# Step sizes with tiles of their own in the second layer of a two-layer kernel

## The chip, the cores and the metric

The kernel runs on one core of a Trainium2 chip. The metric is the device time of one execution in microseconds (us). Five engines work side by side, each through its own list of instructions in order: PE (matmul, with its weight loads shown apart as PEld), DVE (vector work), ACT (activation functions and copies), POOL (a second, slower vector engine) and SP, which here only issues DMAs. An instruction that must wait holds up everything behind it on its engine. SBUF is the on-chip memory of 128 partitions, PSUM the banks that PE writes to.

## What is computed

Two layers run one after the other over x of 16 x 512 x 128. The first holds a state-space mixer and a routed feed-forward part; it is not touched. The second adds to x an attention with hierarchical levels and a recurrent cell over the 16 blocks. What matters here is how the attention forms its step sizes dt and its level weights Lam:

```python
xn = _layernorm(x, axis=-1)
V  = (x @ Wv.T).reshape(Bb, Tt, H, HD)
dl = (x @ Wdl.T).reshape(Bb, Tt, H, LV)
A = -jnp.exp(A_log)
dt = jax.nn.softplus(x @ Wdt.T + dt_bias)
g = A[None, None, :] * dt
Lam = jax.nn.softplus(Lp[None, None] * dl)
cg = jnp.cumsum(g, axis=1)
diff = cg[:, :, None, :] - cg[:, None, :, :]
decay = jnp.exp(jnp.where(tri[None, :, :, None], diff, NEG))
...
Wmat = scores * jnp.transpose(decay, (0, 3, 1, 2)) * jnp.transpose(lam_ts, (0, 2, 1, 3))
Y = jnp.einsum('bhts,bshd->bthd', Wmat, V).reshape(Bb, Tt, H * HD)
```

Here x inside the attention is xn, and lam_ts picks from Lam the level of each pair of positions. There are 16 heads.

## The kernel before

The work is cut into 16 blocks of 512 positions, held as 128 partitions by 4 groups. Blocks of the second layer have tiles named b_..., those of the first layer other names; some first-layer tiles borrow the space of second-layer tiles (lent_...).

The order on each engine is not that of the source. Every operation is recorded by the class Plan, with its dependences, a guessed duration and a base time of its stage. The method flush then walks the list backwards, gives every operation a key (the smaller the more urgent) from its base time and the longest guessed chain behind it, and places operations engine by engine, always the ready one with the smallest key. Two things in the key matter here. First, weights in the tables URGENT and STAGES (in thousands of ns) go by engine and by the name of the tile that is written: "s:b_sp": -3.0 puts off ACT's writes to b_sp, "g:b_sp": 0.5 and "v:b_sp": 1.0 hurry those of POOL and DVE, "v:b_small": -1.0 and, in the stages 16 to 21, "v:b_gr": -8.0 put off DVE's writes to those tiles. Second, each operation gets a random part of up to 50 ns either way from one generator, drawn in that backward walk. All operations are issued from line 479, so the profile shows L479 for all of them, and they are told apart by their tiles.

The second layer's loop (from line 1365 on) runs over the blocks. In one pass block b goes through states, diagonal, products, upper, upper2 and diagonal2, the next block through gates and factors, the one before through finish:

- gates(b), line 978: the projections b_pp (PE) are copied by ACT to vz, whose first 128 columns of each group are V and whose other 176 columns are z. Of these 176, columns 96 to 111 are the step sizes of 16 heads, the other 160 the level weights. V goes out to the DRAM tile dV and comes back in four DMAs as vbd. The softplus of all 176 x 4 = 704 columns is formed in one go: on ACT u = |z|, u = exp(-u), sp = ln(1 + u); on DVE sp = max(z, 0) + sp and z = (u + 1) - 1; on POOL u = u - z and sp = sp + u, a correction for what 1 + u rounds away. For small u the step sizes take a series (ser) in place of the logarithm, put in by a copy_predicated with the mask small. Then gg = dt * A, its three bf16 parts in g3, exp(gg) back into the step columns of sp, and there times a mask tmask.
- factors(b), line 1042: b_pe, 30 small bf16 matmuls per pass that sum g3, then ACT's b_ex = exp(pe); b_la, ten small products of ex and sp on DVE; b_pld, four transposes of sp, from which ACT and DVE make ldr and ld3, and these go through DRAM (dde, dld) to come back as dd and R.
- states(b), line 1125: bv = V * ex, the matmuls b_pG, and a DVE and ACT chain that fills Gs. upper(b, q), line 1166: the matmuls b_pU of four heads with Gs and th_all, copied to b_yq. products(b), line 1233: 16 heads of three matmuls b_pT each, copied by ACT to th_all. diagonal and diagonal2, lines 1207 and 1243: the scans into b_dec, the multiplies by b_pl (from R) and by b_pS, then b_pyd. finish(b), line 1269: the output projection b_po, a layer norm (b_lc_...) and the store.

The tiles of the softplus have one buffer each, vz has two. A new block's tile waits until the block before has read the old one.

Of the kernel before, what the change touches and what calls it, by code (L numbers as in the profile page):

```python
# [12 lines left out]
F32 = mybir.dt.float32  # L13
F32R = mybir.dt.float32r
BF16 = mybir.dt.bfloat16
AF = mybir.ActivationFunctionType
ALU = mybir.AluOpType
# [6 lines left out]
P = 128  # L24
NG = 4
NH = 16
# [56 lines left out]
class Plan:  # L83
# [100 lines left out]
    def act(self, *args, **kw):  # L184
        i = self.record("scalar", "activation", args, kw)
        self.ops[i].deps.add(self.table)
        self.group.append(i)
        return i
# [304 lines left out]
def two_layer_kernel(ctx: ExitStack, tc: tile.TileContext, a: dict, out: bass.AP):  # L493
    nc = Plan(tc.nc, tc)
# [5 lines left out]
    sp = ctx.enter_context(tc.tile_pool(name="s", bufs=1))  # L500
# [7 lines left out]
    def bank(name, tag="tr", shape=(P, 512), dt=F32):  # L508
        return nc.bank(ps, shape, dt, tag, name)

    def bt(shape, dt, tag, name, bufs=None):
        return nc.tile(sp, shape, dt, tag, name, bufs or BUFS.get(tag, 1))

    def wt(shape, dt, name):
        return wp.tile(list(shape), dt, tag=name, name=name)
# [13 lines left out]
    def mm3(o, lh, ll, rh, rl, start=True, stop=True):  # L529
        nc.tensor.matmul(o, lh, rh, start=start, stop=False)  # L530
        nc.tensor.matmul(o, lh, rl, start=False, stop=False)
        nc.tensor.matmul(o, ll, rh, start=False, stop=stop)

    act = nc.act
# [9 lines left out]
    one_c = wt([P, 1], F32, "one_c")  # L544
# [100 lines left out]
    tmask = pk0[:, 134:135]  # L645
# [11 lines left out]
    nA, dtb = rows[:, 0:16], rows[:, 16:32]  # L657
# [35 lines left out]
    for e in range(8):  # L693
# [9 lines left out]
        op=ALU.mult,  # L703
# [264 lines left out]
    def namer1(b):  # L968
        return lambda s: f"b_{s}_{b}"
# [8 lines left out]
    def gates(b):  # L978

        n, d = namer1(b), B[b]  # L980
        xh, xl = d["xh"], d["xl"]
        vz = bt([P, NG, 304], F32, "vz", n("vz"))
        d["V"], z = V, z = vz[:, :, 0:128], vz[:, :, 128:304]
        d["hh"] = hh = bt([P, NG, P], F32, "hh", n("hh"))
        for g in range(NG):
            pp = bank(n(f"pp{g}"), "pj")
            sl = slice(g * P, (g + 1) * P)
            mm3(pp[:, :NP], xh[:, sl], xl[:, sl], wpj_h, wpj_l)
            nc.scalar.copy(vz[:, g, :], pp[:, 0:304])
            if b:  # L990
                nc.vector.tensor_tensor(hh[:, g, :], pp[:, 304:432], cfo[:, g, :], op=ALU.add)
            else:
                nc.vector.tensor_copy(hh[:, g, :], pp[:, 304:432])

        dV = nc.tile(dram, [NG, NG, C, P], F32, "dV", n("dV"), 2)
        nc.sync.dma_start(dV.rearrange("g j s c -> (j s) g c"), V)
        if b < 2:
            vbd.append(bt([P, NG, NG, P], F32, "vbd", n("vbd")))
            nc.vector.memset(vbd[b], 0.0)
        for g in range(NG):  # L1000
            nc.sync.dma_start(vbd[b % 2][g * C : (g + 1) * C, :, g, :], dV[g].rearrange("j s c -> s j c"))

        nc.vector.tensor_tensor(
            z[:, :, 96:112], z[:, :, 96:112], dtb.unsqueeze(1).to_broadcast([P, NG, NH]), op=ALU.add
        )
        u = bt([P, NG, 176], F32, "u", n("u"))
        d["sp"] = sp = bt([P, NG, 176], F32, "sp", n("sp"))
        act(u, z, AF.Abs)
        act(u, u, AF.Exp, scale=-1.0)
        act(sp, u, AF.Ln, bias=one_c)  # L1010
        dtv = sp[:, :, 96:112]

        ud = u[:, :, 96:112]
        ser = bt([P, NG, NH], F32, "ser", n("ser"))
        small = bt([P, NG, NH], mybir.dt.uint8, "small", n("small"))
        nc.vector.tensor_scalar(small, ud, 2.0**-7, None, op0=ALU.is_lt)
        nc.vector.tensor_scalar(ser, ud, 1.0 / 3.0, -0.5, op0=ALU.mult, op1=ALU.add)
        nc.vector.tensor_tensor(ser, ser, ud, op=ALU.mult)
        nc.vector.scalar_tensor_tensor(ser, ser, 1.0, ud, op0=ALU.add, op1=ALU.mult)
        nc.vector.scalar_tensor_tensor(ser, z[:, :, 96:112], 0.0, ser, op0=ALU.max, op1=ALU.add)  # L1020
        nc.vector.scalar_tensor_tensor(sp, z, 0.0, sp, op0=ALU.max, op1=ALU.add)

        nc.vector.tensor_scalar(z, u, 1.0, -1.0, op0=ALU.add, op1=ALU.add)
        nc.gpsimd.tensor_tensor(u, u, z, op=ALU.subtract)
        nc.gpsimd.tensor_tensor(sp, sp, u, op=ALU.add)
        nc.vector.copy_predicated(dtv, small, ser)
        gg = bt([P, NG, NH], F32, "gg", n("gg"))
        nc.vector.tensor_tensor(gg, dtv, nA.unsqueeze(1).to_broadcast([P, NG, NH]), op=ALU.mult)

        g3 = bt([P, 3, NG, NH], BF16, "g3", n("g3"))  # L1030
        gr = bt([P, NG, NH], F32, "gr", n("gr"))
        nc.vector.tensor_copy(g3[:, 0], gg)
        nc.vector.tensor_tensor(gr, gg, g3[:, 0], op=ALU.subtract)
        nc.vector.tensor_copy(g3[:, 1], gr)
        nc.vector.tensor_tensor(g3[:, 2], gr, g3[:, 1], op=ALU.subtract)

        act(dtv, gg, AF.Exp)
        nc.vector.tensor_scalar(dtv, dtv, tmask, None, op0=ALU.mult)

        d["g3"] = g3  # L1040

# [252 lines left out]
    for i in range(-2, NB + 3):  # L1294
# [26 lines left out]
        if i == NB - 1:  # L1321
            gates(0)
            load1(1)
# [39 lines left out]
    for b in range(NB + 1):  # L1363
        nc.base = (NB + 4) * PA + (b + 1) * PB
        nc.start_group(LNEXP)
        if 0 < b < NB:
            states(b)
        if b + 2 < NB:
            load1(b + 2)
        if b + 1 < NB:  # L1370
            gates(b + 1)
        if b:
            finish(b - 1)
        if b < NB:
            if b:
                diagonal(b)
            for q in range(4):
                if b:
                    products(b, heads=range(4 * q, 4 * q + 4))
                if q:  # L1380
                    upper(b, q - 1)
        if b + 1 < NB:
            factors(b + 1)
        if b < NB:
            upper(b, 3)
            upper2(b)
            diagonal2(b)
        if b + 1 < NB:
            nc.start_group(EXPTANH)
            cell_out(b + 1)  # L1390
# [113 lines left out]
```

## Time and profile before

| | |
|---|---|
| Median of 3 runs | 829.51 us (827.62 to 831.28) |
| Profiled execution | 828.71 us |
| Its span, first to last instruction | 826.5 us |
| Granted PE clock, mean | 0.985 |
| First layer, last cell matmuls | up to 328 us |
| Second layer, first b_pp | 276.3 us |
| Second layer, first softplus | 281.3 us |
| Second layer, last softplus | 760.5 us |

The span is the time from the first to the last instruction; the rest of the 828.71 us lies around it. A busy share says how much of the span an engine worked. The chain that ended last is followed back from the last instruction, at each step to what released it. A line of a tile's view gives engine, operation, written and read tiles, count, and the minimum, median and maximum duration in ns, then the first and last start in us and the shape. A line of a chain or timeline gives start and length in us.

### The profile page before, as it was taken

The numbers are of one execution on the slowest core, as the hardware profiler recorded it, in microseconds if no ns is written. First come the engines' busy times: TensorE is split into PE (matmuls) and PEld (weight loads), VectorE is DVE, ScalarE is ACT, GpSimd is POOL, SyncE is SP. The second block draws the span as 40 slices with busy tenths as digits, with TensorE's granted clock in tenths as the row PEclk, the third lists the DMA queues.
The fourth block names the chain that finished last, engine by engine and source line by source line (L and its number), as shares of the span: only waits on it lengthen the run. The fifth ranks groups of instructions, "written<-read, shape, count | busy, mean of one in ns | idle before, by whom it ended". The sixth has DMA issues, their size and how long they took to land.

```text
span 826.5 us, 27744 instructions
## 1 busy us (share of the span) xinstructions
PE 790.8 (96%) x11432; PEld 605.4 (73%) x11432; DVE 735.5 (89%) x1889; ACT 631.9 (76%) x1322; POOL 206.7 (25%) x236
## 2 busy tenths in 40 slices
PE   7899999999999998999999999999999999999994
PEld 4577878777888776787677778768677778677772
DVE  5799999999998996798989999888999989899885
ACT  6788898989898887876696697587588577587573
POOL 2200000000000110333343343533433523433521
PEclk9799999999999998999999999999999999999998
DMA  9516444334333334254345346435346426536311
GB/s 226 132 52 205 141 154 127 103 113 136 112 109 108 109 115 139 78 135 117 104 128 147 96 130 150 130 94 151 100 123 158 136 79 156 130 87 157 88 52 40
DMA packets 92402, 100.18 MB, mean 121 GB/s; under 512 B 26532, under 2 KB 63788, under 8 KB 90156
## 3 DMA queue, kind: packets, MB, share of 16 engines
q1 hardware_dynamic: 92276, 98.41, 42.5%
q8 instruction: 90, 1.47, 0.7%
q14 instruction: 36, 0.29, 0.1%
HBM read 63.70 MB, written 34.67 MB: 119 GB/s over the span
## 4 chain that ended last, share of the span: by engine, by line
PE 56%; DVE 18%; ACT 15%; DMA 4%; issue 3%; POOL 3%; SPq 0%; ACTq 0%; DVEq 0%; POOLq 0%
PE b_pT L479 11%; PE pg L479 6%; DVE b_dec L479 5%; ACT th_all L479 5%; PE b_pU L479 5%; PE po L479 5%; PE pm L479 4%; PE b_pY L479 3%; PE b_pS L479 2%; DVE b_la L479 2%; PE pC L479 2%; ACT L479 2%; PE pxi L479 2%; PE pz L479 2%; PE b_pp L479 2%
## 5 line engine op out<-in xcount | busy, mean ns | idle before, releaser
L479 ACT COPY th_all<-b_pT 128x512 f32<-128x512 f32 x256 | 145.0, 622 | 25.9 <-PE b_pT L479 20.0
L479 PE MATMUL b_pT<-b_xh,A_h 128*128 128x512 f32 x256 | 108.1, 422 | 1.2 <-DVE b_tiles L479 0.9
L479 POOL TENSOR_TENSOR b_u<-b_u,b_vz 128x704 f32<-128x704 f32 x16 | 27.9, 1743 | 298.7 <-DVE b_vz L479 256.9
L479 PE MATMUL b_pT<-b_xh,A_l 128*128 128x512 f32 x256 | 100.8, 394 | 0.0
L479 PE MATMUL b_pT<-b_xl,A_h 128*128 128x512 f32 x256 | 100.4, 392 | 0.0
L479 ACT ACT_TABLE_LOAD x71 | 91.1, 1283 | 1.9 <-PEq L1494 0.7
L479 DVE TENSOR_TENSOR_SCAN b_dec<-b_dd,upat 128x512 f32<-128x512 f32 x64 | 77.8, 1226 | 4.5 <-PE b_pyd L479 3.0
L479 PEld LDWEIGHTS b_pU<-th_all,Gs 128*32 128x32 f32 x4096 | 61.3, 110 | 19.2 <-issue 9.0
L479 PE MATMUL b_pU<-th_all,Gs 128*32 128x64 f32 x4096 | 70.9, 220 | 2.1 <-ACT th_all L479 0.9
L479 PE MATMUL b_pS<-th_all,b_xf 128*32 128x512 f32 x512 | 60.3, 594 | 0.4 <-ACT th_all L479 0.4
L479 PEld LDWEIGHTS b_pT<-b_xh,A_h 128*128 128x128 f32 x256 | 48.1, 188 | 15.3 <-PE b_pT L479 1.3
L479 PEld LDWEIGHTS b_pT<-b_xh,A_l 128*128 128x128 f32 x256 | 48.1, 188 | 10.9
L479 PEld LDWEIGHTS b_pT<-b_xl,A_h 128*128 128x128 f32 x256 | 48.3, 189 | 6.9
L479 ACT COPY b_yq<-b_pU 128x512 f32<-128x512 f32 x64 | 38.5, 614 | 13.8 <-PE b_pU L479 13.4
L479 DVE TENSOR_TENSOR b_dec<-b_dec,b_pl 128x512 f32<-128x512 f32 x64 | 40.3, 680 | 9.4 <-PE b_pl L479 9.4
L479 DVE TENSOR_TENSOR b_dec<-b_pS,b_dec 128x512 f32<-128x512 f32 x64 | 43.6, 681 | 1.2 <-PE b_pS L479 1.0
L479 DVE TENSOR_TENSOR b_la<-b_ex,b_sp 64x32 f32<-64x32 f32 (+3 forms) x160 | 41.4, 284 | 1.7
L479 ACT ACTIVATE lent_vbd_x<-lent_vbd_x,lb_nb,lb_r 128x128 f32<-128x128 f32 x64 | 29.6, 489 | 11.8 <-DVE lb_nb L479 8.7
L479 DVE TENSOR_TENSOR b_aY<-b_pY,b_la 128x384 f32<-128x384 f32 (+1 forms) x64 | 33.9, 543 | 4.4 <-POOL b_ysum L479 3.0
L479 PE MATMUL pg<-lent_yq_x1h,lent_hh_w 128*128 128x512 f32 x96 | 33.8, 431 | 1.1 <-DVE lent_yq_x1h L479 1.1
L479 PE MATMUL pm<-Gs,ww 128*128 128x512 f32 x64 | 34.5, 621 | 0.0
L479 ACT ACTIVATE b_o<-b_o,b_lc_nb,b_lc_r 128x128 f32<-128x128 f32 x64 | 33.7, 552 | 0.9 <-DVE b_lc_nb L479 0.9
(268 smaller groups left out, 2154.7 us busy)
## 6 DMA issues: line engine op xcount, KB each, us to landing
b_dd<-b_dde SPq DMA_DIRECT2D x64, 256.0 KB, 5.7
b_dld<-b_ld SPq DMA_DIRECT2D x48, 96.0 KB, 2.8
b_R<-b_dld SPq DMA_DIRECT2D x16, 288.0 KB
d_x<-lent_vbd_x SPq DMA_DIRECT2D x16, 256.0 KB, 3.4
d_xt<-lent_vbd_x SPq DMA_DIRECT2D x16, 256.0 KB, 3.7
b_xt<-d_xt SPq DMA_DIRECT2D x16, 256.0 KB, 3.7
d_xf<-th_all SPq DMA_DIRECT2D x16, 256.0 KB, 2.0
d_xh<-lent_yq_x1h SPq DMA_DIRECT2D x16, 256.0 KB, 3.6
```

The source lines that it names most:

```text
L479: o.inst = getattr(getattr(self.nc, o.eng), o.name)(*o.args, **o.kw)
```

## The change

The step sizes get tiles of 64 columns: zd for the biased input, ud for exp(-|zd|), dtv for the softplus. Their three ACT functions, the max-and-add and the correction are recorded before those of the 704 columns, and their correction is on DVE. The softplus of all 704 columns stays as it was, the step columns among them, but z no longer gets the bias, and the step columns of sp are overwritten at the end by exp(gg) times the mask. gg and gr lose their own tiles and use zd and ud. The series, the mask small, g3 and everything outside gates stay as they were.

```diff
-        nc.vector.tensor_tensor(
-            z[:, :, 96:112], z[:, :, 96:112], dtb.unsqueeze(1).to_broadcast([P, NG, NH]), op=ALU.add
-        )
-        u = bt([P, NG, 176], F32, "u", n("u"))
-        d["sp"] = sp = bt([P, NG, 176], F32, "sp", n("sp"))
-        act(u, z, AF.Abs)
-        act(u, u, AF.Exp, scale=-1.0)
-        act(sp, u, AF.Ln, bias=one_c)
-        dtv = sp[:, :, 96:112]
-
-        ud = u[:, :, 96:112]
+
+        zd = bt([P, NG, NH], F32, "zd", n("zd"))
+        nc.vector.tensor_tensor(zd, z[:, :, 96:112], dtb.unsqueeze(1).to_broadcast([P, NG, NH]), op=ALU.add)
+        ud = bt([P, NG, NH], F32, "ud", n("ud"))
+        dtv = bt([P, NG, NH], F32, "dtv", n("dtv"))
+        act(ud, zd, AF.Abs)
+        act(ud, ud, AF.Exp, scale=-1.0)
+        act(dtv, ud, AF.Ln, bias=one_c)
+
...
-        nc.vector.scalar_tensor_tensor(ser, z[:, :, 96:112], 0.0, ser, op0=ALU.max, op1=ALU.add)
-        nc.vector.scalar_tensor_tensor(sp, z, 0.0, sp, op0=ALU.max, op1=ALU.add)
-
-        nc.vector.tensor_scalar(z, u, 1.0, -1.0, op0=ALU.add, op1=ALU.add)
-        nc.gpsimd.tensor_tensor(u, u, z, op=ALU.subtract)
-        nc.gpsimd.tensor_tensor(sp, sp, u, op=ALU.add)
+        nc.vector.scalar_tensor_tensor(ser, zd, 0.0, ser, op0=ALU.max, op1=ALU.add)
+        nc.vector.scalar_tensor_tensor(dtv, zd, 0.0, dtv, op0=ALU.max, op1=ALU.add)
+
+        nc.vector.tensor_scalar(zd, ud, 1.0, -1.0, op0=ALU.add, op1=ALU.add)
+        nc.vector.tensor_tensor(ud, ud, zd, op=ALU.subtract)
+        nc.vector.tensor_tensor(dtv, dtv, ud, op=ALU.add)
         nc.vector.copy_predicated(dtv, small, ser)
-        gg = bt([P, NG, NH], F32, "gg", n("gg"))
+        gg, gr = zd, ud
         nc.vector.tensor_tensor(gg, dtv, nA.unsqueeze(1).to_broadcast([P, NG, NH]), op=ALU.mult)
...
-        gr = bt([P, NG, NH], F32, "gr", n("gr"))
...
         act(dtv, gg, AF.Exp)
-        nc.vector.tensor_scalar(dtv, dtv, tmask, None, op0=ALU.mult)
+
+        u = bt([P, NG, 176], F32, "u", n("u"))
+        d["sp"] = sp = bt([P, NG, 176], F32, "sp", n("sp"))
+        act(u, z, AF.Abs)
+        act(u, u, AF.Exp, scale=-1.0)
+        act(sp, u, AF.Ln, bias=one_c)
+        nc.vector.scalar_tensor_tensor(sp, z, 0.0, sp, op0=ALU.max, op1=ALU.add)
+        nc.vector.tensor_scalar(z, u, 1.0, -1.0, op0=ALU.add, op1=ALU.add)
+        nc.gpsimd.tensor_tensor(u, u, z, op=ALU.subtract)
+        nc.gpsimd.tensor_tensor(sp, sp, u, op=ALU.add)
+        nc.vector.tensor_scalar(sp[:, :, 96:112], dtv, tmask, None, op0=ALU.mult)
```

## The prediction

> **What bounds the kernel now.** I read first the busy shares and the chain that ended last, both over the whole span of 826.5 us.
>
> ```profile
> PE 790.8 (96%) x11432; PEld 605.4 (73%) x11432; DVE 735.5 (89%) x1889; ACT 631.9 (76%) x1322; POOL 206.7 (25%) x236
> ...
> PE 56%; DVE 18%; ACT 15%; DMA 4%; issue 3%; POOL 3%; SPq 0%; ACTq 0%; DVEq 0%; POOLq 0%
> ```
>
> The reader is to see that PE carries most of the chain, DVE is nearly as full, and POOL, which the change relieves of a place in a chain and not of work, holds 3%. The changed code runs from about 281 us on, so the second view is the steady part of the second layer, twelve blocks of 31 us.
>
> ```profile
> 382.00:754.00 372.00, 364.14 (x7275) 279.69 (x7275) 338.20 (x831) 273.08 (x546) 150.44 (x174) 1.00 0.48 127
> ```
>
> The columns are length, then busy PE, weight loads, DVE, ACT and POOL. PE is idle for 372 - 364.1 = 7.9 us in twelve blocks. Whatever a shorter chain brings here, it can bring about 8 us. DVE is busy 338.2 / 372 = 91%, ACT 73%. The clock is 1.00. So the steady part has little to win and an engine, DVE, that has little room for more.
>
> Third, the chain of waits where the second layer starts, which does run through the step-size chain:
>
> ```profile
> 345.50 1.71 POOL b_u L479
> ...
> 347.29 1.72 POOL b_sp L479
> ...
> 349.03 0.25 DVE b_sp L479
> ...
> 349.30 0.24 DVE b_gg L479
> ...
> 350.33 0.62 PE b_pld L479 x4
> ```
>
> The two full-width POOL operations end at 349.01, six pieces of DVE work follow, and PE goes on at 350.33. Adding such pieces over the whole chain, POOL's b_u and b_sp hold 3.4 + 3.4 us in two blocks near 345 and 370 us, and 5.4 us in the rest: 12.3 us.
>
> Last, the rows that price the edit, from the view of single tiles (minimum, median and maximum ns).
>
> ```profile
> L479 ACT ACTIVATE b_u<-b_vz x16: 791/822/883, 281.3 to 760.5; 128x704 f32<-128x704 f32 x16
> L479 POOL TENSOR_TENSOR b_sp<-b_sp,b_u x16: 1684/1707/2037, 289.1 to 771.3; 128x704 f32<-128x704 f32 x16
> L479 ACT ACTIVATE b_sp<-b_gg x16: 256/257/258, 292.8 to 774.5; 128x64 f32<-128x64 f32 x16
> L479 DVE TENSOR_TENSOR b_gr<-b_gg,b_g x16: 194/212/226, 295.1 to 774.7; 128x64 f32<-128x64 f32 x16
> L479 DVE SCALAR_TENSOR_TENSOR b_ser<-b_vz,b_ser x16: 192/216/226, 285.5 to 767.5; 128x64 f32<-128x64 f32 x16
> L479 DVE TENSOR_SCALAR b_ser<-b_u x16: 160/190/201, 283.3 to 762.9; 128x64 f32<-128x64 f32 x16
> L479 DVE COPY_PREDICATED b_sp<-b_small,b_ser x16: 202/236/1296, 292.2 to 773.5; 128x64 f32<-128x64 uint8 x16
> ```
>
> **The change part by part.** *Nothing full-width goes away.* The three ACT functions over 704 columns, the 704-column DVE pair and both POOL operations stay, and the bias add, the series, the casts and the mask multiply keep their number; 7 operations per block come on top. No DMA is added or moved between queues; b_dV and the four vbd loads need only the ACT copies of b_pp, as before.
>
> *ACT gets Abs, Exp and Ln over 64 columns.* Abs and Exp at 257 ns (row b_sp<-b_gg). Ln carries a bias column; the only small pair is b_lc_r, where Ln with one takes 303 ns and Exp without 211, so 257 + 92 = 349. Per block 0.86 us, for 16 blocks 13.8 us. The cover is ACT's idle time, (372 - 273.1) / 12 = 8.2 us a block. Without that cover ACT's busy share decides. Bounds: 0, and 73% of 13.8 = 10.1 us. I take the 16% that ACT holds of the chain between 382 and 754 us (58 of 372 us, its pieces added): 2.2 us.
>
> *DVE gets four operations over 64 columns:* the max-and-add 0.216, the add-one-take-one 0.190, and the two that were part of POOL's 704 columns, 0.212 each. Together 0.83 us a block, 13.3 us in all. *And they meet POOL.* Ten small DVE operations that came after the POOL pair can now run beside it. What that costs shows here:
>
> ```profile
> 464.81 1.69 POOL L479 TENSOR_TENSOR b_sp<-b_sp,b_u 128x704 f32<-128x704 f32 x1
> 464.88 2.17 DVE L479 TENSOR_TENSOR b_o<-b_o,b_x 128x512 f32<-128x512 f32 x1
> ```
>
> The DVE operation, 0.68 us in the median, takes 2.17 us beside the POOL one. Small ones stretch too: the copy_predicated row has 202 ns at best, 1296 at worst, and a mean of 628 between 382 and 693 us. Bounds: nothing, or two full collisions a block at 1296 - 202 = 1.09 us, 35 us. I take one mean stretch per block, 0.43 x 16 = 6.8 us, since the list of DVE instructions interleaves the small ones with PSUM reads.
>
> The Trainium skill, page "SBUF — State Buffer", section "Who interferes with whom", says that a DVE instruction with two SBUF inputs and a POOL instruction lock each other out, and the loser blocks for the whole instruction. The b_o line agrees in kind. Were each of the two 1.7 us POOL operations to cost DVE half its length, that rule would make it 1.7 x 16 = 27 us in place of 6.8, and at the share of a third used below the sum would be 6.8 us higher.
>
> So DVE has 13.3 + 6.8 = 20.1 us more. How much reaches the end? At least the share that DVE holds of the chain in the steady part, 75 of 372 us, 20%; at most its busy share, 91%. Nearer the first, because the chain shows where time went, but above it, because the added work makes DVE fuller: a third, 6.7 us.
>
> *The waits.* Here the built order of instructions matters. In 15 of 16 blocks the full-width Ln still stands ahead of the small one on ACT. On DVE the mask multiply, which now writes into sp and so waits for POOL's b_sp, stands ahead of the last of the three g3 operations in 15 of 16 blocks, ahead of the first in 10. Behind a waiting mask multiply stand those g3 operations, and behind them PE's b_pe, ACT's b_ex and DVE's b_bv. The factors' chain is freed from POOL in the data and tied to it again by the queue. What remains is that b_pld needs only the mask multiply after POOL: in place of 349.01 to 350.33 about 0.3 us, 1.0 us less. In the two blocks near 345 and 370 us where the chain runs there: -2.0 us. Bounds: 0, and -10.8 us, which is all 12.3 us of POOL less 3.5 blocks of two 0.21 us replacements.
>
> *The rest of the order moves too.* PE's first b_pU of a block stood after 13 of its 16 products in eleven blocks and now stands after all 16 in fourteen; b_pG stands nearly three products later on the average. PE changes between full and 32-row or 32-column tiles 196 times in place of 187. Such a change cost about 0.14 us (one pair of them, around the 32 b_pU matmuls at 485.56 us, put 0.28 us into the row of matmuls): 1.3 us, at least 0.
>
> Sum: 6.7 + 2.2 - 2.0 + 1.3 = 8.2 us. The profiled execution took 828.7 us, 0.8 below the median of 829.5 shown; on the one it gives 836.9, on the other 837.7. I forecast 837.
>
> **The rivals.** *The cover holds.* The 2.8 us of DVE idle time and 8.2 of ACT in each block take the added work, and PE keeps its 98%. For it: PE waits for b_g only 4.4 us in six blocks. Against it: DVE's longest waits, 9.4 us before the b_pl multiplies, lie after the place where most of the small operations run. Time: 829.5, give or take 3.
>
> *Faster.* The POOL pair leaves the path of b_pe. Place: the blocks whose chain now runs POOL b_u, b_sp. It decides once POOL is done before DVE reaches the mask multiply, so that this holds up nothing. Price: -10.8, with the ACT and switch terms + 3.5: 829.5 - 7.3 = 822. For it: ACT waits 32.8 us for b_gg over 16 blocks, and b_gg no longer needs POOL. Against it: the DVE order above, and the 7.9 us of idle PE.
>
> *PE starves.* With all four b_pU groups behind the last product, PE has nothing to put in when Gs or b_g is late, and waits once a block as long as its longest wait for b_g, 1.6 us: 13 blocks x 1.6 = 21 us, 850. Against it: between b_pG and the first b_pU lie as many products as before, so Gs isn't asked for sooner.
>
> *The change is only a reordering.* Its chain doesn't come ahead, and the time is set by new random parts in the priorities, which shift the first layer too. That layer's PE is busy 198.9 of 200 us between 60 and 260 us, so this can cost and hardly gain; I count it into the forecast and the first rival.
>
> **How the numbers follow.** Forecast, slower by 4 to 16 us: 0.46. (4: DVE at its 20%, 4.0, with ACT 2.2 and the gain -2.0. 16: DVE and ACT midway between their bounds, 11.1 and 6.2, with 1.3 and -2.0.) PE starves: 0.13. The cover holds: 0.27. Faster: 0.14. A run to run spread of 827.6 to 831.3 us lets a measurement tell about 0.5%, 4.1 us, from nothing: faster means under 825.4 us, slower over 833.7. Range 825 to 847: it leaves out most of the faster case and the upper part of the starved one; the forecast's own range is 834 to 846. Chances: faster 0.14, within 0.27, slower 0.59.
>
> **What would show it.** Right: DVE busy 13 to 25 us longer, ACT 12 to 15, POOL the same; PE's idle time between 382 and 754 us grows from 7.9; small DVE operations with maxima over 1 us beside POOL; b_g's last operation still after POOL's b_sp. Wrong: b_g done well before b_sp and b_pe earlier in each block; PE's idle time unchanged; a loss that lies in the first layer or between 262 and 382 us, where I put none.

## The result and the profile after

The changed kernel takes **862.18 us** (median of 4 runs, 861.61 to 863.03) against 829.50 for the kernel before in the same comparison. The ratio is 1.0395, with a 95% interval of 1.037 to 1.042. It is slower by 32.7 us; the forecast was slower by 8, and the range ended at 847. The profiled span is 860.8 us against 826.5.

The first view is that of the busy shares and of the chain that ended last, over the whole span of the changed kernel.

```profile
PE 806.4 (94%) x11431; PEld 615.1 (71%) x11432; DVE 758.3 (88%) x1953; ACT 643.4 (75%) x1370; POOL 214.3 (25%) x236
...
PE 40%; DVE 36%; ACT 12%; DMA 5%; issue 4%; POOL 1%; SPq 1%; ACTq 0%; DVEq 0%; POOLq 0%
```

DVE is busy 22.8 us longer (758.3 - 735.5) and ACT 11.5, much as the added instructions say; POOL, which got no work, 7.6. But the chain has turned over: DVE's part of it doubled from 18% to 36%, PE's fell from 56% to 40%. PE is idle 54.4 us of the span, not 35.7, and its same 11,432 matmuls (one record is missing from this profile) hold it 15.6 us longer. 18.7 + 15.6 is the whole of the 34.3 us of span.

Now the same stretches as before, first the first layer, then the steady part of the second. Columns: length, then busy PE, weight loads, DVE, ACT and POOL, clock, DMA share, GB/s.

```profile
60.00:260.00 200.00, 198.59 (x1187) 155.23 (x1186) 192.22 (x536) 176.61 (x404) 1.29 (x1) 1.00 0.40 130
382.00:754.00 372.00, 353.11 (x6982) 270.59 (x6975) 331.44 (x825) 265.79 (x545) 145.24 (x163) 0.99 0.44 119
```

The first layer is untouched: PE 198.6 of 200 us, as before (198.9). In the steady part PE's idle time went from 7.9 to 18.9 us, and DVE is busy *less* of this window than before (331.4 against 338.2), though it has more to do: it waits, and the window now holds less of the work (6982 matmuls in place of 7275). PE's longest waits, over the whole span, have other names than before:

```profile
PE b_pU L479 <- DVE Gs L479: 5.4, 9, 1.7
PE b_pU L479 <- issue: 3.0, 5, 0.9
PE b_pe L479 <- DVE b_g L479: 2.9, 2, 1.9
```

The columns are the sum in us, how often, and the longest. b_pU's wait for Gs, 0.4 us before between 300 and 800 us, is now the first of them. The wait of b_pe for b_g, 4.4 us in six blocks before, is down to 2.9 in two. So the step sizes make PE wait less often now, and something behind them makes it wait more. The profile puts only 5.4 of the 54.4 us of idle time down to Gs by name, so this points to a place and is no account of the whole loss.

When b_bv of a block starts on DVE tells where the time is lost. After minus before, in blocks 0 to 15: -3.4, 5.2, 8.8, 16.3, 16.6, 20.5, 22.2, 25.0, 25.7, 25.6, 26.9, 31.0, 30.9, 31.8, 33.4, 37.7 us. It is spread over the layer, with a first jump: by block 3 16.3 of the 37.7 us are lost. In the chain of waits just before that, in the third block:

```profile
404.41 0.56 DVE b_t L479
404.96 4.48 DVE b_dec L479 x3
409.45 0.45 DVE Gs L479
...
410.23 0.21 DVE b_hh L479
...
410.49 0.97 PE b_pT L479 x3
411.46 0.56 PE b_pU L479 x29
```

Three scans into b_dec, 4.48 us, stand on DVE between the step b_t of the recurrence and the Gs that is formed from it. PE stands still only 0.8 us there, and for b_hh, which comes on DVE behind this Gs; until then it had products to do. The experiments below led back to these scans. But in this block they don't tell the two kernels apart: in the third block of the kernel before four scans, 4.9 us, stand ahead of the last Gs too, but there the chain that ended last runs over PE's products and goes on to b_pU at 398.09 us without a wait.

### The profile page after: what moved, and what is told of

It reads as the page before. It is cut to its first block, busy times and chain, and to the rows that moved or that the text cites. A ratio compares the mean times of both kernels' runs of the same rounds, so it can differ in the third digit from the quotient of the medians.

```text
span 860.8 us, 27860 instructions
## 1 busy us (share of the span) xinstructions
PE 806.4 (94%) x11431; PEld 615.1 (71%) x11432; DVE 758.3 (88%) x1953; ACT 643.4 (75%) x1370; POOL 214.3 (25%) x236
## 4 chain that ended last, share of the span: by engine, by line
PE 40%; DVE 36%; ACT 12%; DMA 5%; issue 4%; POOL 1%; SPq 1%; ACTq 0%; DVEq 0%; POOLq 0%
DVE b_dec L479 9%; PE b_pT L479 7%; PE pg L479 5%; PE b_pU L479 4%; PE po L479 4%; ACT th_all L479 3%; PE b_pS L479 3%; DMA b_dd<-b_dde 3%; DVE Gs L479 3%; DVE th_all L479 3%; PE pm L479 2%; DVE b_ser L479 2%; PE b_pY L479 2%; ACT L479 2%; DVE b_la L479 2%
## 5 line engine op out<-in xcount | busy, mean ns | idle before, releaser
L479 ACT COPY th_all<-b_pT 128x512 f32<-128x512 f32 x256 | 143.1, 614 | 54.1 <-PE b_pT L479 30.1
L479 PE MATMUL b_pU<-th_all,Gs 128*32 128x64 f32 x4096 | 75.8, 223 | 11.7 <-DVE Gs L479 5.4
L479 PEld LDWEIGHTS b_pU<-th_all,Gs 128*32 128x32 f32 x4096 | 63.4, 111 | 31.6 <-issue 12.7
L479 PEld LDWEIGHTS b_pT<-b_xh,A_h 128*128 128x128 f32 x256 | 48.4, 189 | 16.3 <-ACT th_all L479 3.7
L479 DVE TENSOR_TENSOR b_aY<-b_pY,b_la 128x384 f32<-128x384 f32 (+1 forms) x64 | 33.9, 547 | 13.9 <-PE b_pY L479 8.6
L479 POOL TENSOR_TENSOR b_ld<-b_ldr,b_ld 96x512 bf16<-96x512 f32 x16 | 20.4, 1278 | 99.7 <-DVE b_ld L479 66.7
L479 POOL TENSOR_TENSOR b_ysum<-b_aY 128x128 f32<-128x128 f32 x60 | 30.7, 519 | 22.0 <-DVE b_aY L479 21.6
L479 PE MATMUL b_pY<-pk,b_yq 128*128 128x128 f32 x256 | 35.8, 280 | 0.1
L479 DVE TENSOR_TENSOR b_la<-b_ex,b_sp 64x16 f32<-64x16 f32 (+3 forms) x160 | 34.2, 238 | 1.8
```

Of the source, the lines that this page charges most:

```text
L479: o.inst = getattr(getattr(self.nc, o.eng), o.name)(*o.args, **o.kw)
```

## The experiments

Every ratio is to the kernel before on the same chip (medians of 826.6 to 830.1 us). The expectations say TensorE, VectorE, ScalarE and GpSimd for PE, DVE, ACT and POOL. Four theories were written down: **ORDER** (the loss is in the new order of instructions), **WORK** (in the added instructions), **DRAW** (in the random parts of the priorities, which the change deals anew), **COLLISION** (in small DVE operations that run beside POOL's wide pair).

### The old order with the new work, and the new order with less work

For e1 the planner's list is replaced by the list of the kernel before, each added operation right behind its full-width counterpart:

```
+        rank = struct.unpack(...)          # position of each operation
+        order = sorted(ops, key=lambda o: rank[o.idx])
         with self.tc.manual_schedule():
```

In the third block of this list the mask small is formed behind the subtraction, so the series is put in for all step sizes there; the instructions are the same. e2 keeps the changed kernel's list and doesn't issue the four operations:

```
-        nc.vector.scalar_tensor_tensor(dtv, zd, 0.0, dtv, op0=ALU.max, op1=ALU.add)
-        nc.vector.tensor_scalar(zd, ud, 1.0, -1.0, op0=ALU.add, op1=ALU.add)
-        nc.vector.tensor_tensor(ud, ud, zd, op=ALU.subtract)
-        nc.vector.tensor_tensor(dtv, dtv, ud, op=ALU.add)
```

> The changed computation, but every operation stands where it stood in the kernel before; the seven added ones of a block stand right behind their full-width counterparts (each small ACT function behind the wide one, the four small DVE operations behind the wide max-and-add and the wide add-one-take-one). No new priorities. Theory ORDER (the loss is what the scheduler made of the new graph): 829 to 838 us, the 0.8 us of DVE and 0.9 us of ACT a block mostly covered. Theory WORK (the added operations and their collisions with POOL fill DVE): 850 to 862 us. If the earlier step sizes are worth something by themselves: below 829.

> The changed kernel in its own order with the four added DVE operations of the step sizes left out (max-and-add, add-one-take-one, subtract, add), so that dt is only ln(1 + exp(-|z|)). Nothing else moves. ORDER: 855 to 862 us, the loss stays. WORK: the loss shrinks by what DVE gets back, 0.8 us a block and the collisions with it, to 840 to 850 us.

e1: 847.02 us, ratio 1.0189 (1.0142 to 1.0236). e2: 863.08, ratio 1.0406 (1.0348 to 1.0465). Both theories are half wrong. The work costs 17.7 us in the old order, and in the new order taking its DVE part away gives nothing. The new order alone costs as much as the whole change.

### Other draws

> The kernel before with another seed of the random part of the priorities (4 in place of 3). Theory DRAW (the loss is a new draw of the random parts, which shift because operations were added): 845 to 865 us, as far off as the change. ORDER through the graph alone, with the draw of no weight: 826 to 834 us. In between, the draw is a part.

> The changed kernel with another seed (6 in place of 3). DRAW: the time moves by 10 us or more against 862, and could come near 830. ORDER through the graph alone: 858 to 866 us.

```
-JIT, SEED = 50.0, 3
+JIT, SEED = 50.0, 4      (e3: before;  e4: after, with 6)
```

Before with seed 4 takes 835.98 us, ratio 1.008 (1.0051 to 1.0109); after with seed 6 takes 846.15, ratio 1.0202 (1.0173 to 1.0232). A draw is worth up to 16 us, so one pair of kernels doesn't tell what the change does. Later runs filled this in: e7 and e8 with the random part set to zero (JIT 0.0), e16 to e18 with more seeds.

> The kernel before, with the random part of the priorities set to zero. Beside the next run it removes the draw from the comparison. DRAW (the change moves the draw of the random parts, and the 32.7 us are mostly bad luck): this run and the next differ by less than 10 us. ORDER (the priorities that the planner works out from the changed graph are worse by themselves): the next run is slower than this one by 15 us or more. This run by itself: 832 to 846 us, since the draw of before was picked from several.

> The changed kernel, with the random part of the priorities set to zero. DRAW: within 10 us of the run before it, so about 835 to 850 us. ORDER: 15 us or more over the run before it, so 850 to 870 us.

> The changed kernel with seed 8 of the random part. DRAW (the result is largely the seed's): anything between 836 and 866 us, with the mean of the changed kernel's four draws so far (862.2, 846.2, 858.5 without a random part, and this) within 12 us of that of before's (829.3, 836.0, 836.6). PRIORITIES: 848 to 864 us, the mean 18 us or more above that of before.

> The kernel before with seed 6 of the random part, to stand beside the changed kernel with the same seed (846.2 us). LUCK (the draw of before was a good one, by some 6 us): 833 to 840 us, as with seed 4 (836.0) and without a random part (836.6). DRAW (the two kernels have the same spread of draws, and the comparison is mostly chance): 842 us or more.

> The kernel before with seed 8, beside the changed kernel's 856.7 us. LUCK: 833 to 840 us, and a mean of the four pairs' differences of 18 to 25 us. DRAW: 842 us or more, and a mean difference under 15 us.

| random part | before, us (ratio) | after, us (ratio) | after / before |
|---|---|---|---|
| seed 3 | 829.5 (1) | 862.18 (1.0395) | 1.0395 |
| seed 6 | 839.30 (1.0144) | 846.15 (1.0202) | 1.0057 |
| seed 8 | 839.84 (1.0145) | 856.69 (1.0324) | 1.0176 |
| none | 836.61 (1.0074) | 858.46 (1.0359) | 1.0283 |

The mean of the last column is 1.0228, so **the change as such costs about 18.9 us**. This mean of few draws is not sharp: taken from the spread of the four draws of the changed kernel and the five of the kernel before (seed 4 among them), its 95% interval is some 10 us either way. By the same mean the other 13.8 of the 32.7 are the draw: seed 3 was the best of five for the kernel before (0.9% under the mean of its four above, 7.5 us) and the worst of four for the changed one (6.2 us). In all four pairs the changed kernel is the slower one, and its fastest draw (846.15) lies above the slowest of the kernel before (839.84). An equal seed doesn't give the two kernels equal random parts, since the changed one draws for more operations. The pair with none is the only one without a draw, and there the change costs 21.9 us.

### Is it the collision with POOL?

In e1 the addition into dtv, placed right behind the operation that releases POOL, met POOL's full-width subtraction in every block. The first line is e1's, from the view of single tiles:

```profile
L745 DVE TENSOR_TENSOR b_dtv<-b_dtv,b_ud x16: 1592/1604/1735, 287.1 to 788.6; 128x64 f32<-128x64 f32 x16
```

1.60 us in the median for what takes 0.21 in the changed kernel, in 16 of 16 blocks: 22 us. The three figures of the line are minimum, median and maximum in ns. e5 puts the three correction operations ahead of the wide pair, e6 the rest of the step sizes' DVE work too, up to g3. In both lists the wide maximum of the third block stands behind the add-one-take-one, so its level weights differ.

> The changed operations in the order of before, as in the first experiment, with one difference: the three correction operations of the step sizes on VectorE (add one and take one, the subtraction, the addition) stand ahead of VectorE's two wide operations that release GpSimd, and not behind them, so none of them can meet GpSimd's wide subtraction. COLLISION (what the first experiment lost, 17.7 us, is the addition held up by GpSimd for 1.6 us in each block): the addition takes 0.2 to 0.3 us, VectorE's busy time falls by some 20 us against the first experiment, and the time is 829 to 837 us; what is left over 829.3 is the price of the added work. WORK (the added instructions themselves, seven in each block, cost the time wherever they stand): 842 to 850 us again, with the busy time down.

> As the run before it, and in addition the whole of the step sizes' VectorE work (the masked copy, the product with the decay rates, and the four operations that make the three-part split) stands ahead of the two wide operations that release GpSimd; TensorE's, ScalarE's and the DMAs' order is that of before. This is the change as its words describe it: the step sizes finished before the level weights, without the reordering. If the split's wait on GpSimd cost anything in the kernel before, its end comes some 3 us earlier in each block and the time is 820 to 830 us. RIVAL (nothing waited on it: PE's order sets when it is used, and the pair on GpSimd starts 1.5 us later in each block): 831 to 842 us.

```profile
L745 DVE TENSOR_TENSOR b_dtv<-b_dtv,b_ud x16: 224/226/227, 286.7 to 784.8; 128x64 f32<-128x64 f32 x16
```

In e5, whose line this is, the stall of that operation is gone, and the time isn't: 846.32 us, ratio 1.019 (1.0156 to 1.0225), DVE busy 762.4 against 765.8 us in e1. Other DVE operations meet POOL in its place; the masked copy has a mean of 743 ns in e5 and of 449 in e1. e6 is worse, 858.15 us, ratio 1.0343 (1.029 to 1.0395). POOL's pair starts later there, and the mask multiply behind it is what PE's b_pld needs (e6's waits between 300 and 800 us):

```profile
PE b_pld L745 <- DVE b_sp L745: 17.2, 11, 3.1
```

So my expectation of a gain from finishing the step sizes first fell. With PE's order fixed, what e6 did earlier for b_pe made b_pld late.

e9 tried the same in the *new* order: small functions ahead of the wide ones on ACT, the small DVE operations ahead of the wide maximum. In the changed kernel's own list the small maximum stands ahead of the wide add-one-take-one in 5 blocks of 16 only.

> The changed kernel in its own order, with one thing moved: in each block the step sizes' three functions stand directly before the level weights' same functions on ScalarE, and VectorE's nine small operations on them (the series, the maximum, the correction) before VectorE's wide maximum; so the step sizes are truly formed first, which in the changed kernel's order is so in 5 blocks of 16 only. Nothing is left out. COLLISION (in the changed kernel the small operations run beside GpSimd's wide pair, because the planner put them behind the wide ones that release it: VectorE's operations beside GpSimd take 54.5 us longer in all than the same operations elsewhere, against 33.3 us before): that sum falls to 30 to 40 us and the time to 840 to 852 us. REST (the loss lies in how the recurrence's products, tiles and transfers were reordered, and VectorE's delays only fill its waits): the sum falls and the time stays at 855 to 865 us.

The count of time lost beside POOL (each second-layer DVE operation against the median of its like without POOL) fell from about 55 to about 34 us as COLLISION said, DVE's busy time fell by 9.0 us to 749.3, and the kernel took 882.12 us, ratio 1.0648 (1.0609 to 1.0688), 20 more. e9 is another list too, so this alone doesn't clear the collisions. But across lists the count doesn't go with the time: e12 below has about 48 us of it and takes 828.64. That speaks against COLLISION as the main cause. And e9's longest waits of PE (first line, between 300 and 800 us) and of DVE (second) name the recurrence again:

```profile
PE b_pU L745 <- DVE Gs L745: 10.7, 5, 3.0
```

```profile
DVE b_dec L745 <- PE b_pl L745: 19.5, 10, 3.5
```

### What the work costs, on ACT and on DVE

> The fifth experiment (the changed operations in the order of before, the correction ahead of the wide operations), with the four added VectorE operations left out: the step sizes are the plain ln(1+exp(-|z|)), without the maximum and the correction of the rounding. ScalarE's three added functions stay. VECTORE (the four operations, on an engine that is 89% busy, cost the 16 us of the fifth experiment): 828 to 835 us. SCALARE (the three small functions, which delay the wide exponential and logarithm by 0.86 us in each block, cost them): 840 to 847 us. Between the two, the shares are read from it.

e12 is e5, in the same list, without the four DVE operations of e2's diff. It takes 828.64 us, ratio 1.0003 (0.9984 to 1.0023). ACT's three added functions cost nothing that this interval shows, although they delay the wide Ln, and the four DVE operations cost all of e5's loss: 846.32 - 828.64 = 17.7 us, or 15.5 by the two ratios, since e5 and e12 ran on different chips. DVE's busy time is 19.7 us longer (762.4 - 742.7). One of PE's waits shows part of how. e5 first, then e12, between 270 and 820 us:

```profile
PE b_pe L745 <- DVE b_g L745: 10.8, 15, 1.9
```

```profile
PE b_pe L748 <- DVE b_g L748: 3.9, 4, 1.9
```

With the added work b_g is late 15 times, without it 4 times, and PE waits 6.9 us longer for it.

e12 also gives the cleanest answer to ORDER. It issues the same instructions as e2; only the list differs. In the changed kernel's list they take 863.08 us, in e5's, which keeps the order of the kernel before, 828.64. So the order alone is worth 33 us by the ratios, 34 by the times, as much as the whole loss.

### Whose priorities?

In the changed kernel's list of priorities not only the step sizes moved. What lies behind them (b_pe, b_bv, b_pG, Gs, b_pU, b_pY) became less urgent, while the path of the level weights (b_pld, b_ldr, the transfers dde, dd and R) and most scans kept their priority. The next runs give the operations their old or new priorities and let the planner make the list, as it always does:

```
             o.key += rng.uniform(-JIT, JIT)
+            o.key = float(KEYS[o.idx])
```

> The changed kernel, ordered by the planner as always, but with every operation's priority as it was in the kernel before (an added operation has that of the operation it was split from). PRIORITIES (the split shortens the chain behind the step sizes, the planner then takes them, and what hangs on them, for less urgent, and that makes the order worse): 828 to 842 us, most of the 32.7 us gone. WORK (the seven added instructions in a block cost 17 us wherever they stand, as in both runs in the old order): 845 to 850 us. DRAW (any other order is worse than the one of before): 850 to 865 us.

> The kernel before, with the priorities that the changed kernel's operations have for everything outside the step sizes and level weights; no instruction is added. PRIORITIES (the new priorities of the rest make a worse order by themselves): 845 to 860 us. RIVAL (they do harm only through the split operations' own place, beside GpSimd): 828 to 840 us.

> The changed kernel, where only the operations of the step sizes and level weights (28 in a block) have their priorities as before, an added one that of the operation it was split from; all others keep the changed kernel's. SPLIT (the split operations' own lower urgency is what hurts, since they come late and hold up the recurrence behind them): 840 to 848 us, near the 841.8 of the tenth run. REST (the loss of urgency of everything else is what hurts): 854 to 864 us. BOTH in equal parts: 848 to 854 us.

> The reverse of the run before it: the 28 operations of a block keep the changed kernel's priorities, and everything else has that of before. SPLIT: 854 to 864 us. REST: 840 to 848 us. BOTH: 848 to 854 us.

> The tenth run (all priorities as before), in the same order, with the four added VectorE operations left out: the step sizes are the plain ln(1+exp(-|z|)), without the maximum and the correction of the rounding. WORK (what the old priorities leave of the loss is the added VectorE work, at its full price as in the order of before): 826 to 832 us. DRAW (it is that the order is another one): 838 to 843 us.

| run | priorities of the split operations | of the rest | us | ratio (95%) |
|---|---|---|---|---|
| after | new | new | 862.18 | 1.0395 (1.037 to 1.042) |
| e13 | old | new | 856.85 | 1.034 (1.029 to 1.039) |
| e14 | new | old | 847.15 | 1.022 (1.0178 to 1.0262) |
| e10 | old | old | 841.80 | 1.0154 (1.0136 to 1.0173) |
| e15, four DVE operations left out | old | old | 838.96 | 1.0116 (1.0076 to 1.0157) |
| e11, no operation added | - | new | 841.90 | 1.0156 (1.013 to 1.0182) |

The old priorities give back 20.4 us: those of the rest 15.0, those of the split operations 5.3. Each row is one list, and a draw moved the time by up to 16 us, so the parts are not sharp. Nor are they priorities alone: the values put in hold the random parts that each kernel drew with seed 3, so "old" brings the best draw of the kernel before with it and "new" the worst of the changed one. From the other side, the kernel before with the rest's new priorities and nothing added loses 12.6 us (841.90 - 829.27), ratio 1.0156; a mere other draw of it goes up to 1.0145, so this supports the sign only weakly. That the planner's priorities by themselves make the worse order is supported best by the pair without a random part, 836.61 against 858.46 us, though the added work is in that pair too. e15 answers the question left by e10: the added work costs 2.8 us in that list, within the two runs' intervals, and the rest of e10's loss is that the list is another one; the five draws of the kernel before lie between 829.5 and 839.8.

The chains of e13 and e14 stand for all of them. First e13, rest new:

```profile
DVE 37%; PE 37%; ACT 12%; DMA 6%; issue 4%; SPq 1%; POOL 1%; DVEq 0%; ACTq 0%; POOLq 0%
```

Then e14, rest old:

```profile
PE 67%; DVE 19%; ACT 7%; DMA 3%; issue 2%; POOL 1%; SPq 1%; ACTq 0%; DVEq 0%; POOLq 0%
```

In every list that the planner made with the rest's new priorities DVE holds 29% to 37% of the chain; with its old ones 12% to 25%.

### What the new priorities do

Here are the scans and the Gs operations of the fifth block on DVE, from the timeline (start and length in us). Before:

```profile
441.94 0.69 DVE L479 TENSOR_TENSOR b_bv<-b_vz,b_ex 128x512 f32<-128x512 f32 x1
...
451.01 0.54 DVE L479 TENSOR_TENSOR Gs<-b_tiles,b_t 128x384 f32<-128x384 f32 x1
...
451.98 0.29 DVE L479 TENSOR_TENSOR Gs<-Gs,b_t 128x128 f32<-128x128 f32 x1
...
453.79 1.23 DVE L479 TENSOR_TENSOR_SCAN b_dec<-b_dd,upat 128x512 f32<-128x512 f32 x1 [1.28 <-PE b_pyd L479]
```

After:

```profile
458.54 1.68 DVE L479 TENSOR_TENSOR b_bv<-b_vz,b_ex 128x512 f32<-128x512 f32 x1
...
467.09 1.23 DVE L479 TENSOR_TENSOR_SCAN b_dec<-b_dd,upat 128x512 f32<-128x512 f32 x1 [0.42 <-DMA b_dd<-b_dde]
468.24 0.53 DVE L479 TENSOR_TENSOR Gs<-b_tiles,b_t 128x384 f32<-128x384 f32 x1
468.69 3.45 DVE L479 TENSOR_TENSOR_SCAN b_dec<-b_dd,upat 128x512 f32<-128x512 f32 x3
...
472.57 0.28 DVE L479 TENSOR_TENSOR Gs<-Gs,b_t 128x128 f32<-128x128 f32 x1
```

Before, the last Gs is formed 10.0 us after b_bv and the scans follow. After, four scans (1.23 + 3.45 us) go first, one of them with a wait for its transfer, and the last Gs comes 14.0 us after b_bv. b_pU needs that Gs, and in the built order it stands behind all the products, with none of them left to fill PE when Gs is late. In this block it isn't late: PE has products until 474.4 us and goes on to b_pU without a wait. The nine waits for Gs, 5.4 us, lie in other blocks. That the late Gs is what put b_pU behind the products is my reading; no run moved the scans alone.

Counted in this way, in how many of blocks 0 to 14 more than 4 us of scans stand between b_bv and the last Gs, and how long after b_bv that Gs starts in the mean:

| run | us | blocks of 15 | last Gs, us |
|---|---|---|---|
| before | 829.5 | 4 | 13.1 |
| before, seed 4 / none / 6 / 8 | 836.0 / 836.6 / 839.3 / 839.8 | 6 / 6 / 5 / 3 | 13.8 / 13.9 / 13.2 / 12.7 |
| e15, e10 (all old priorities) | 839.0 / 841.8 | 3 / 3 | 12.8 / 13.0 |
| e11 (before, rest new) | 841.9 | 9 | 16.0 |
| after, seed 6 | 846.2 | 11 | 15.9 |
| e14 (rest old) | 847.2 | 8 | 15.3 |
| after, seed 8; e13; after, none | 856.7 / 856.9 / 858.5 | 12 / 11 / 15 | 17.0 / 17.4 / 17.9 |
| after; e2 | 862.2 / 863.1 | 14 / 14 | 17.6 / 17.7 |

Among the lists that the planner made, few blocks (3 to 6) go with 829 to 842 us, many (11 to 15) with 846 to 863, and the two between (8 and 9) with 842 and 847. e2 has the same list as after without the four operations, and the same count and time. Within the first group the count doesn't order the times. This is a regularity over fifteen kernels, not an experiment on the scans alone: a list that differs from the changed kernel's only in where the scans stand wasn't run. Nor can the scans be the whole of it. In blocks 0 to 2 the kernel before has 4.8 to 4.9 us of them ahead of the last Gs as well (4.8 to 6.0 after), and just there the first 16.3 us are lost; what costs them stays open. The later blocks, of which ten of twelve differ in this, hold the other 21.4 us. In the old order (e1, e5, e6) the count is 4, as before, and the loss there is the work.

## Why the prediction was wrong

**What bounds the kernel**: right. The steady part had little to win, and DVE had no room.

**ACT's three functions**, 13.8 us of work and 2.2 on the path: busy +11.5, and 0 on the path, give or take 2, where it could be measured alone (e12, 1.0003). In the upper end of the forecast ACT's 6.2 is midway between 2.2 and 10.1, not between the bounds that I had given, 0 and 10.1; that would be 5.0.

**DVE's four operations and POOL**, 20.1 us: well sized, +22.8 in the changed kernel and +19.7 between e12 and e5. The share that reaches the end, "a third", was wrong both ways: 15.5 to 17.7 of 19.7 us, 80% to 90%, in the old order, about nothing in the new one (e2 against after), 2.8 us in e10's. The bounds, 20% and 91%, held one of these, and the third that I took met none. Within the term, the mean stretch beside POOL was taken at 0.43 us a block; full stalls of 1.6 us occur (e1). The Trainium skill's page "SBUF — State Buffer", section "Who interferes with whom", has it that a DVE instruction with two SBUF inputs contends with a POOL instruction that reads SBUF, and that the port pair which they share is an exclusive lock; e1's addition, 1.60 us beside POOL's 1.69, agrees. How many stalls occur differs from order to order, and e9 shows that fewer of them can go with a longer time.

**The waits**: right that DVE's mask multiply ties the end of g3 to POOL, but this priced a gain of 2.0 us in a list that no longer had the same critical path. In the changed kernel's chain POOL holds 1%, and b_pld still waits for DVE, 2.5 us in five blocks.

**"The rest of the order moves too", 1.3 us: this is the step that failed.** I saw that b_pU had gone behind all products in fourteen blocks and that b_pG came later, and priced only the change of tile shapes on PE. I didn't ask what had pushed b_pU back, nor what the same instructions would cost in the new order. Measured, the new order alone costs 33.7 us in this draw (e2, 0.0406 x 829.5; much the same against e12, the same instructions in the old order) and, over four pairs of draws, the whole change about 18.9. What goes with it in the traces is DVE's order: scans of over 4 us ahead of the last Gs in 14 of 15 blocks in place of 4. That these scans are the cause is argued and not shown, and the loss up to block 3 isn't theirs.

**The rivals.** "PE starves" had the right place, b_pU behind the last product, and with 850 us was the nearest. My argument against it was that between b_pG and b_pU as many products lie as before. That counts what covers the wait on PE and leaves out that Gs itself came 4.5 us later after b_bv (17.6 against 13.1), behind other work on DVE. And its 21 us were to be waits of PE for Gs or b_g; the profile shows 5.4 and 2.9. "Only a reordering" I held able to shift the first layer alone, and gave it no price. It needed one, and the second layer was the place.

**What would show it**: DVE and PE's idle time changed as I had said, and b_g's last operation does start behind POOL's b_sp in all 16 blocks. ACT's 11.5 us lie just under the 12 to 15, and POOL, which should have stayed the same, is busy 7.6 us longer. The sign I named as proof against me, a loss between 262 and 382 us, is there: PE's idle time in it goes from 4.2 to 9.0 us.

What stays open: what in the new order costs the first 16.3 us, which of the rest's priorities puts the scans ahead of Gs, and how much of the 18.9 us a planner that kept them behind would save. None of the variants of the change beat the kernel before; the nearest, e12, equals it and leaves the correction out.

## What to carry to other kernels

Where a planner orders the instructions by the longest chain behind them, splitting an operation can change the priority of everything that hangs on it. Put the same instructions into the old and the new order and measure that difference before you price the instructions themselves, and read the built order of the busiest in-order engine for a long operation that has slipped ahead of the recurrence. Compare several draws of both kernels before you credit or blame the change: here the draw made some 13.8 of 32.7 us. And don't price added work on a nearly full engine by its share of the chain: in a fixed order it cost 80% to 90% of its length, in a list with waits in it nothing.

## What the hardware showed

A 64-column DVE addition took 1.60 us, not 0.21, in sixteen of sixteen blocks beside POOL's 1.69 us subtraction (e1), and moving it away (e5) took only 3.4 us from DVE's busy time, since other operations were stalled in its place. The other surprise is PE: the same 11,432 matmuls kept it busy for 806.4 us in place of 790.8. The granted clock has a large part in that. It was 1.00 in most of the span and 0.50 in a few stretches; in these PE was busy for 34.3 us after and 15.2 before. In such a stretch 64 matmuls of b_pU took 1.94 us, elsewhere 1.10. If half of PE's time there is counted as lost, which is an estimate, the 19.1 us more make some 9.5 of the 15.6. Two of the new stretches, at 395.1 and 511.1 us, begin within 2 us of the end of a wait of PE, of 2.1 and 1.7 us. In the mean the clock fell from 0.985 to 0.971, and to 0.960 in e9, the slowest run; it doesn't follow the idle time alone, for e6, with 56.9 us of it, has 0.981.
